# Gates by seven block products in a two-layer graph network kernel, with block sums on GpSimd

## Chip, cores, metric

The kernel runs on one core of a Trainium2 chip. The metric is device time in microseconds, from the core's first to its last instruction; most executions agree within 0.3%. SBUF is the on-chip memory that holds the tiles; PSUM is the one into which TensorE's results go (tiles named ps_). A change of over 2% counts as faster or slower.

## The reference

There are 64 graphs of 256 nodes with 256 features, in fp32. Layer 0, cut to what matters, is a gated update of x. Its inputs are a convolution along the nodes and a message sum:

```python
x_conv = relu(h + xc)                       # two convolutions, the second with 17 taps
x_nmp  = A @ relu(x @ w_msg.T + b_msg)      # A = exp(-dist) * mask
x_in = concatenate([x_conv, x_nmp])         # (256, 512)
gi = x_in @ w_ih.T + b_ih                   # (256, 768), parts r, z, n
gh = x @ w_hh.T + b_hh
r = sigmoid(gi_r + gh_r); z = sigmoid(gi_z + gh_z)
nn_ = tanh(gi_n + r * gh_n)
out = (1 - z) * nn_ + z * x                 # then x = layernorm(x + out)
```

Layer 1 normalizes (the kernel calls that result h), projects, sums over neighbours and normalizes again.

## The kernel before

Graphs are handled in turns, one graph k a turn, in batches of eight. A turn also holds pieces of its neighbours: message sums of k+1, distances of k+2, messages of k+3, projection and aggregation of k-1. `pump()` inserts pieces of the next batch's convolution at ten places of a turn. In these traces each engine runs its instructions in the order of the program. The gates, which the change rewrites:

```python
def gates_rz(k, n):                          # n: half of the nodes
    prz = bank("ps_rz")                      # 512 columns: r and z
    for c in range(C):
        nc.tensor.matmul(prz, XT[k][:, c, q], whh[:, c, 0:2 * D], start=(c == 0), stop=False)
    for i, t in enumerate(ins):              # xc (2 chunks), nmp (2 chunks)
        nc.tensor.matmul(prz, t, wih[:, i, 0:2 * D], start=False, stop=(i == 3))
    nc.vector.tensor_add(rz[:, n, :], prz, brzn[:, :2 * D])
    nc.scalar.activation(rz[:, n, :], rz[:, n, :], AF.Tanh, scale=0.5)
# gates_n(k, n): the same with 256 columns for each of the two n parts, and one addition

def update(k):                               # ... statistics of w on VectorE, small powers on GpSimd
    for n in range(C):
        nc.vector.tensor_scalar(H[k][:, n, :], w[:, n, :], mv[:, n, 0:1], q[:, 1, n:n + 1],
                                ALU.subtract, ALU.mult)
    # ... X1 by two ScalarE activations

for k in range(b * BG, (b + 1) * BG):        # a turn, cut
    load(k + 3); load_x(k + 1)               # the transfers, at its start
    gates_rz(k, 0); pump(); gates_n(k, 0); pump()
    transposes_h(k - 1); pump(); gates_rz(k, 1); pump(); passing(k + 1); pump()
    factors(k + 2); gates_n(k, 1); pump(); project(k - 1)
    # ... update(k), distances(k + 2), messages(k + 3), mask(k + 2), aggregate(k - 1)
```

## Time and profile before

| | before |
|---|---|
| time, median of 4 runs | 2313.66 us |
| TensorE busy | 2225 us, 96% |
| VectorE busy | 1685 us, 73% |
| GpSimd busy | 469 us, 20% |
| a turn without convolution work for TensorE | 25.6 us |
| a batch of eight turns | 272 us |

The lines themselves stand in the prediction. "Busy" is time in which an engine runs instructions. Idle time matters only on the engine that bounds a stage, so shares are read by stage, here by turn. A group's line gives its instructions' total busy time, their mean in ns, and the idle time before them with what ended it.

I measure turns from one start of the transposes of h on TensorE to the next. The heavy stage is the first six of the eight intervals so cut in a batch, where VectorE carries most of the next convolution; the light stage is the other two.

### The profile page before, as it was taken

Reading aid. Unit: us, or ns where it says so; the run is one execution under the profiler, and the core shown is the slowest. Engines: PE = TensorE matmul, PEld = TensorE weight load, DVE = VectorE, ACT = ScalarE, POOL = GpSimd, SP = SyncE. Lnnn points to the kernel's source line nnn. Section 1 sums busy time; section 2 is a strip of 40 time slices with the busy share of each in tenths; the row PEclk is TensorE's granted clock in tenths of the full one; section 3 lists DMA queues with packets and bytes.
Section 4 is the critical chain, followed back from the end, with each engine's and each line's share of the span. In section 5 each row is a group of like instructions: output and inputs, shape, how many; then the busy total and the mean of one; then the engine's idle time right before and its main releaser. Section 6 shows DMA issues by size and latency. Waiting matters only on the chain.

```text
span 2314.6 us, 24215 instructions
## 1 busy us (share of the span) xinstructions
PE 2225.2 (96%) x8262; PEld 1456.2 (63%) x8262; DVE 1685.2 (73%) x3212; ACT 766.0 (33%) x1577; POOL 468.7 (20%) x925
## 2 busy tenths in 40 slices
PE   7879999999999999999999999999999999999996
PEld 4565566666666666666666566665666656666663
DVE  2893998759794788829887498956889398874543
ACT  4514222442224321353224332253223532243332
POOL 1000221312122222202212131221222122121211
PEclk8998999999999999999999999999999999999998
DMA  5543152224323144221532234222433214321100
GB/s 176 156 161 114 59 170 67 85 94 130 118 73 109 50 137 132 74 100 37 169 99 73 101 106 143 75 96 69 136 105 101 94 43 151 113 78 37 46 23 14
DMA packets 211128, 226.66 MB, mean 98 GB/s; under 512 B 22087, under 2 KB 201790, under 8 KB 211006
## 3 DMA queue, kind: packets, MB, share of 16 engines
q1 hardware_dynamic: 188448, 191.14, 26.2%
q10 hardware_dynamic: 22558, 33.99, 4.2%
q8 instruction: 66, 1.08, 0.2%
q14 instruction: 56, 0.46, 0.1%
HBM read 179.22 MB, written 45.88 MB: 97 GB/s over the span
## 4 chain that ended last, share of the span: by engine, by line
PE 69%; DVE 21%; DMA 4%; issue 3%; POOL 2%; ACT 1%; ACTq 0%; SPq 0%; DVEq 0%; POOLq 0%
PE ps_rz L637 14%; PE ps_k L383 12%; DVE XF L103 8%; PE ps_n L649 7%; PE ps_rz L635 7%; PE ps_out L712 6%; PE ps_c L454 5%; PE ps_nmp L619 4%; PE ps_n L647 4%; PE ps_out L724 3%; PE ps_msg L575 3%; DVE w L103 2%; DVE XF L464 2%; DVE bst L654 2%; DMA w<-w2m 2%
## 5 line engine op out<-in xcount | busy, mean ns | idle before, releaser
L103 DVE SCALAR_TENSOR_TENSOR XF<-XF 128x512 f32<-128x512 f32 (+2 forms) x800 | 506.7, 664 | 7.0
L676 POOL TENSOR_SCALAR q<-mv 128x2 f32<-128x2 f32 x64 | 32.1, 502 | 1459.1 <-DVE mv L655 1459.1
L383 PE MATMUL ps_k<-w,XF 128*128 128x256 f32 x1316 | 302.1, 385 | 15.2 <-ACT AT L609 11.6
L383 PEld LDWEIGHTS ps_k<-w,XF 128*128 128x128 f32 x1316 | 248.5, 192 | 64.1 <-ACT AT L609 17.3
L650 DVE TENSOR_TENSOR gn<-ps_n,brzn 128x512 f32<-128x512 f32 x128 | 88.1, 688 | 239.4 <-PE ps_n L649 239.4
L641 ACT ACTIVATE rz<-rz 128x512 f32<-128x512 f32 x128 | 80.7, 631 | 509.9 <-DVE rz L640 509.9
L635 PE MATMUL ps_rz<-whh,xT 128*128 128x512 f32 x512 | 240.8, 592 | 0.0
L637 PE MATMUL ps_rz<-wih,xc 128*128 128x512 f32 x512 | 240.6, 592 | 0.0
L637 PE MATMUL ps_rz<-wih,nmp 128*128 128x512 f32 x512 | 240.6, 592 | 0.0
L712 PE MATMUL ps_out<-wrr,hT 128*128 128x512 f32 x512 | 232.8, 598 | 5.5 <-ACT hT L701 5.5
L640 DVE TENSOR_TENSOR rz<-ps_rz,brzn 128x512 f32<-128x512 f32 x128 | 87.2, 681 | 192.2 <-PE ps_rz L637 192.2
L637 PEld LDWEIGHTS ps_rz<-wih,nmp 128*128 128x128 f32 x512 | 97.3, 190 | 122.5 <-issue 122.5
L637 PEld LDWEIGHTS ps_rz<-wih,xc 128*128 128x128 f32 x512 | 97.2, 190 | 122.5 <-issue 121.5
L712 PEld LDWEIGHTS ps_out<-wrr,hT 128*128 128x128 f32 x512 | 98.1, 192 | 105.2 <-issue 89.6
L580 ACT ACTIVATE msg<-msg 128x512 f32<-128x512 f32 x64 | 40.4, 631 | 353.1 <-DVE msg L579 353.1
L575 PE MATMUL ps_msg<-wms,xT 128*128 128x260 f32 x512 | 134.1, 402 | 12.5 <-DMA adj<-in_adjT_dram 8.1
L635 PEld LDWEIGHTS ps_rz<-whh,xT 128*128 128x128 f32 x512 | 92.2, 190 | 64.5 <-issue 61.2
L647 PE MATMUL ps_n<-whh,xT 128*128 128x256 f32 x512 | 131.6, 379 | 0.0
L649 PE MATMUL ps_n<-wih,xc 128*128 128x256 f32 x512 | 131.4, 379 | 0.0
L649 PE MATMUL ps_n<-wih,nmp 128*128 128x256 f32 x512 | 131.4, 379 | 0.0
L360 DVE TENSOR_TENSOR XF<-XF 128x512 f32<-128x512 f32 (+3 forms) x128 | 125.2, 1004 | 1.8
L454 PE MATMUL ps_c<-xTc,w 128*128 128x512 f32 x256 | 118.1, 604 | 7.6 <-ACT xTc L446 7.6
(105 smaller groups left out, 3486.6 us busy)
## 6 DMA issues: line engine op xcount, KB each, us to landing
w<-w2m SPq DMA_DIRECT2D x105, 768.0 KB, 5.9
xn<-in_x_dram SPq DMA_DIRECT2D x32, 512.0 KB, 4.3
xt<-xTc ACTq DMA_DIRECT2D x32, 512.0 KB, 3.3
xT<-xt SPq DMA_DIRECT2D x64, 256.0 KB, 3.0
adj<-in_adjT_dram SPq DMA_DIRECT2D x64, 256.0 KB, 2.8
x<-in_x_dram SPq DMA_DIRECT2D x64, 256.0 KB, 3.1
xb<-in_x_dram SPq DMA_DIRECT2D x32, 512.0 KB, 4.9
out_dram<-y ACTq DMA_DIRECT2D x64, 256.0 KB, 2.2
```

The costliest lines, as they stand in the source:

```text
L103: nc.vector.scalar_tensor_tensor(o, in0, s, in1, op0=op0, op1=op1)
L360: (nc.vector.tensor_add if add else nc.vector.tensor_sub)(sl(o, n), sl(a, n), sl(b, n))
L383: nc.tensor.matmul(ps, X[:, slot, c * P:(c + 1) * P], w(m, c), start=(c == 0), stop=(c == C - 1))
L454: nc.tensor.matmul(ps, w1[:, c, o * P:(o + 1) * P], xTc[:, c, :], start=(c == 0), stop=(c == C - 1))
L575: nc.tensor.matmul(ps[:, :D + 4], XT[k][:, c, m * P:(m + 1) * P], wms[:, c, :], start=(c == 0), stop=(c == C - 1))
L619: nc.tensor.matmul(ps[:, d * N:(d + 1) * N], MSG[k][:, m, d * P:(d + 1) * P], AT[k][:, m, :], start=(m == 0), stop=(m == C - 1))
L635: nc.tensor.matmul(prz, XT[k][:, c, q], whh[:, c, 0:2 * D], start=(c == 0), stop=False)
L637: nc.tensor.matmul(prz, t, wih[:, i, 0:2 * D], start=False, stop=(i == 3))
L647: nc.tensor.matmul(pn[:, D:], XT[k][:, c, q], whh[:, c, 2 * D:], start=(c == 0), stop=(c == C - 1))
L649: nc.tensor.matmul(pn[:, :D], t, wih[:, i, 2 * D:], start=(i == 0), stop=(i == 3))
L650: nc.vector.tensor_add(RZ[k][1][:, n, :], pn, brzn[:, 2 * D:])
L712: nc.tensor.matmul(ps, hT[:, c, n * P:(n + 1) * P], wrr[:, c, :], start=(c == 0), stop=(c == C - 1))
```

## The change

The gates become a 2 x 2 block product over node halves and feature chunks, done with seven products in place of eight (a Strassen-type scheme: four sums of blocks on each side come first, and save one product). The weights' sums are made once. The left sums are made per graph on GpSimd, for x, xc and nmp. A product has 384 columns (a third each of r, z and n) for nmp and xc, and 256 for x. Bank sums replace some additions. h moves from VectorE to ScalarE. To make room, x is updated in place and the ring of xc is shorter; the loads move from the start of a turn to its middle.

```diff
+    def blocks(src, s1, s2, s3, s4):
+        a11, a12, a21, a22 = (src[:, c, n * P:(n + 1) * P] for n in range(C) for c in range(C))
+        nc.gpsimd.tensor_add(s1, a21, a22)
+        nc.gpsimd.tensor_sub(s2, s1, a11)
+        nc.gpsimd.tensor_sub(s3, a11, a21)
+        nc.gpsimd.tensor_sub(s4, a12, s2)
+        return a11, a12, s4, a22, s1, s2, s3
 ...
+        a = bank("ps_a")
+        block_product(k, 0, a, True)
+        nc.scalar.copy(g00, a[:, :HG])
+        d = bank("ps_d")
+        block_product(k, 1, d, True)
+        nc.vector.tensor_add(g00, g00, d[:, :HG])
+        nc.gpsimd.tensor_add(g00, g00, bg[:, 1, :])
 ...  (products 4 and 6 into banks b_ and c_)
+        block_product(k, 5, a, False)
+        nc.vector.tensor_add(g.rearrange("p n h e -> p (n h) e")[:, 1:3, :],
+                             a[:, :HG].unsqueeze(1).to_broadcast([P, 2, HG]), bg)
+        nc.gpsimd.tensor_add(g11, g11, g01)
 ...  (product 2 onto b_, added into g01; product 3 onto c_, added into g10; tanh after each)
-        for n in range(C):
-            nc.vector.tensor_scalar(H[k][:, n, :], w[:, n, :], mv[:, n, 0:1], q[:, 1, n:n + 1],
-                                    ALU.subtract, ALU.mult)
+        for i, dst in ((1, H[k]), (0, w)):
+            for n in range(C):
+                nc.scalar.activation(dst[:, n, :], w[:, n, :], AF.Identity, ...)
 ...
+            load(k + 3); load_adj(k + 2); load_x(k + 1)      # after the third gate step
```

More of the change, by code (lines that the diff above doesn't have):

```diff
@@ L31 @@
 NB = B // BG
+RING = 10
+HG = 3 * P
 PI = math.pi
@@ L128, in gnn_two_layers @@
     tb_dram = nc.inline_tensor(np.ascontiguousarray(tb), name="tap_matrix")
-    tap_sb = const.tile([TAPS * OB, NM * OB], F32)
-    nc.scalar.dma_start(out=tap_sb, in_=tb_dram.ap())
     mhalf = const.tile([P, 8], F32)
@@ L169, in filters @@
     def filters(pool):
+        tap_sb = pool.tile([TAPS * OB, NM * OB], F32, name="tap_sb")
+        nc.scalar.dma_start(out=tap_sb, in_=tb_dram.ap())
         W2[0] = pool.tile([P, C, NM, D], F32, name="w2all")
@@ L520, in conv @@
             yield cost(2)
-        xcs = [work.tile([P, C, 4, N], F32, tag="xc", name="xc", bufs=3) for _ in range(2)]
+        if "xc" not in XC:
+            XC["xc"] = work.tile([P, RING, C, N], F32, name="xc", bufs=1)
+        ring, at = XC["xc"], b * BG % RING
+        spans = [(0, min(BG, RING - at), at)]
+        if spans[0][1] < BG:
+            spans.append((spans[0][1], BG, 0))
         def channels(q):
@@ L529, in channels @@
                 pv = ps.rearrange("p (j g t) -> p j g t", j=4, g=BG)
-                for h in range(2):
+                for g0, g1, r in spans:
                     nc.scalar.activation(
-                        xcs[h][:, o].rearrange("p g (t j) -> p j g t", j=M)[:, 4 * q:4 * q + 4],
-                        pv[:, :, 4 * h:4 * h + 4, :], AF.Relu)
+                        ring[:, r:r + g1 - g0, o].rearrange("p g (t j) -> p j g t", j=M)[:, 4 * q:4 * q + 4],
+                        pv[:, :, g0:g1, :], AF.Relu)
                 yield 1.0
@@ L548, in conv, with load_adj @@
         for g in range(BG):
-            XC[b * BG + g] = (xcs[g // 4], g % 4)
-    XG, ADJ, XT, NMP, AT, MSG, X1, H, ST, RZ, OUTS = ({} for _ in range(11))
+            XC[b * BG + g] = ring[:, (b * BG + g) % RING]
+    XG, ADJ, XT, NMP, AT, MSG, X1, H, ST, G, GN, LEFT, OUTS = ({} for _ in range(13))
     def load(k):
-        if k >= B:
-            return
-        XT[k] = work.tile([P, C, N], F32, tag="xT", name="xT", bufs=4)
-        nc.sync.dma_start(out=XT[k], in_=xt_dram[k // 2][:, :, (k % 2) * N:(k % 2 + 1) * N])
-        ADJ[k] = work.tile([P, C, N], F32, tag="adj", name="adj", bufs=5)
-        nc.sync.dma_start(out=ADJ[k], in_=adjT[k].rearrange("(c p) n -> p c n", p=P))
+        if k < B:
+            XT[k] = work.tile([P, C, N], F32, tag="xT", name="xT", bufs=4)
+            nc.sync.dma_start(out=XT[k], in_=xt_dram[k // 2][:, :, (k % 2) * N:(k % 2 + 1) * N])
+    def load_adj(k):
+        if k < B:
+            ADJ[k] = work.tile([P, C, N], F32, tag="adj", name="adj", bufs=4)
+            nc.sync.dma_start(out=ADJ[k], in_=adjT[k].rearrange("(c p) n -> p c n", p=P))
     def load_x(k):
         if k < B:
-            XG[k] = work.tile([P, C, D], F32, tag="x", name="x")
+            XG[k] = work.tile([P, C, D], F32, tag="x", name="x", bufs=3)
             nc.sync.dma_start(out=XG[k], in_=x[k].rearrange("(c p) d -> p c d", p=P))
     def messages(k):
-        MSG[k] = work.tile([P, C, D], F32, tag="msg", name="msg", bufs=3)
+        MSG[k] = work.tile([P, C, D], F32, tag="msg", name="msg")
         st = sts[k % len(sts)]
@@ L621, in passing @@
         nc.scalar.copy(NMP[k].rearrange("p c n -> p (c n)"), ps)
-    def inputs(k, n):
-        xc, g = XC[k]
-        q = slice(n * P, (n + 1) * P)
-        return q, (xc[:, 0, g, q], xc[:, 1, g, q], NMP[k][:, 0, q], NMP[k][:, 1, q])
-    def gates_rz(k, n):
-        if n == 0:
-            RZ[k] = (work.tile([P, C, 2 * D], F32, tag="rz", name="rz", bufs=1),
-                     work.tile([P, C, 2 * D], F32, tag="gn", name="gn", bufs=1))
-        q, ins = inputs(k, n)
-        prz = bank("ps_rz")
-        for c in range(C):
-            nc.tensor.matmul(prz, XT[k][:, c, q], whh[:, c, 0:2 * D], start=(c == 0), stop=False)
-        for i, t in enumerate(ins):
-            nc.tensor.matmul(prz, t, wih[:, i, 0:2 * D], start=False, stop=(i == 3))
-        rz = RZ[k][0]
-        nc.vector.tensor_add(rz[:, n, :], prz, brzn[:, :2 * D])
-        nc.scalar.activation(rz[:, n, :], rz[:, n, :], AF.Tanh, scale=0.5)
@@ L643, in gates_n @@
-    def gates_n(k, n):
-        q, ins = inputs(k, n)
-        pn = bank("ps_n")
-        for c in range(C):
-            nc.tensor.matmul(pn[:, D:], XT[k][:, c, q], whh[:, c, 2 * D:], start=(c == 0), stop=(c == C - 1))
-        for i, t in enumerate(ins):
-            nc.tensor.matmul(pn[:, :D], t, wih[:, i, 2 * D:], start=(i == 0), stop=(i == 3))
-        nc.vector.tensor_add(RZ[k][1][:, n, :], pn, brzn[:, 2 * D:])
+    def blocks(src, s1, s2, s3, s4):
[5 more added lines that the diff above has]
+        return a11, a12, s4, a22, s1, s2, s3
@@ new lines, in sums, with block_product @@
+    def sums(k, name):
+        if name == "x":
+            src = XT[k]
+            t = work.tile([P, 4, P], F32, name="xsum", bufs=1)
+            s3 = t[:, 3, :]
+        else:
+            src = {"nmp": NMP, "xc": XC}[name][k]
+            t = work.tile([P, 3, P], F32, name=name + "sum", bufs=1)
+            s3 = src[:, 0, P:]
+        LEFT[k, name] = blocks(src, t[:, 0, :], t[:, 1, :], s3, t[:, 2, :])
+    def block_product(k, i, ps, start):
+        for j, (name, w) in enumerate((("nmp", wg[:, i, 1, :]), ("x", wx[:, i, :]), ("xc", wg[:, i, 0, :]))):
+            nc.tensor.matmul(ps[:, :w.shape[-1]], LEFT[k, name][i], w, start=start and j == 0, stop=j == 2,
+                             skip_group_check=not start)
@@ new lines, in gates @@
+    def gates(k):
+        g = work.tile([P, C, 2, HG], F32, name="g", bufs=1)
+        G[k] = g
+        g00, g01, g10, g11 = (g[:, n, h, :] for n in range(C) for h in range(2))
+        a = bank("ps_a")
[5 more added lines that the diff above has]
+        nc.gpsimd.tensor_add(g00, g00, bg[:, 1, :])
+        yield
+        b_ = bank("ps_b")
+        block_product(k, 4, b_, True)
+        nc.scalar.copy(g11, b_[:, :HG])
+        c_ = bank("ps_c")
+        block_product(k, 6, c_, True)
+        nc.vector.tensor_add(g11, g11, c_[:, :HG])
+        yield
+        block_product(k, 5, a, False)
+        nc.vector.tensor_add(g.rearrange("p n h e -> p (n h) e")[:, 1:3, :],
+                             a[:, :HG].unsqueeze(1).to_broadcast([P, 2, HG]), bg)
+        nc.gpsimd.tensor_add(g11, g11, g01)
+        yield
+        block_product(k, 2, b_, False)
+        nc.vector.tensor_add(g01, g01, b_[:, :HG])
+        nc.scalar.activation(g[:, 0, :, :2 * P], g[:, 0, :, :2 * P], AF.Tanh, scale=0.5)
+        yield
+        block_product(k, 3, c_, False)
+        nc.vector.tensor_add(g10, g10, c_[:, :HG])
+        nc.scalar.activation(g[:, 1, :, :2 * P], g[:, 1, :, :2 * P], AF.Tanh, scale=0.5)
+        yield
@@ L652, in stats, with gates_n @@
+    def gates_n(k):
+        ps = bank("ps_n")
+        for n in range(C):
+            for c in range(C):
+                nc.tensor.matmul(ps[:, n * D:(n + 1) * D], XT[k][:, c, n * P:(n + 1) * P], wn[:, c, :],
+                                 start=(c == 0), stop=(c == C - 1))
+        GN[k] = work.tile([P, C, D], F32, name="gn", bufs=1)
+        nc.vector.tensor_add(GN[k], ps.rearrange("p (n d) -> p n d", n=C), bn_.unsqueeze(1).to_broadcast([P, C, D]))
     def stats(mv, k, src):
@@ L657, in update @@
     def update(k):
-        rz, gn = RZ[k]
-        nn = work.tile([P, C, D], F32, tag="nn", name="nn", bufs=1)
-        stt(nn, rz[:, :, :D], 1.0, gn[:, :, D:], op0=ALU.add, op1=ALU.mult)
-        stt(nn, nn, 0.5, gn[:, :, :D])
+        g, w, nn = G[k], XG[k], GN[k]
+        parts = nn.rearrange("p n (h e) -> p n h e", h=2)
+        stt(nn, g[:, :, 0, :2 * P], 1.0, nn, op0=ALU.add, op1=ALU.mult)
+        stt(parts, parts, 0.5, g[:, :, :, 2 * P:])
         nc.scalar.activation(nn, nn, AF.Tanh)
         yield
-        w = work.tile([P, C, D], F32, tag="w", name="w", bufs=1)
-        nc.vector.tensor_sub(w, XG[k], nn)
-        stt(w, rz[:, :, D:], 3.0, w, op0=ALU.add, op1=ALU.mult)
+        nc.vector.tensor_sub(w, w, nn)
+        stt(w, g[:, :, 1, :2 * P], 3.0, w, op0=ALU.add, op1=ALU.mult)
         stt(w, nn, 4.0, w)
@@ L678, in update @@
         nc.gpsimd.tensor_tensor(q, q, mhalf[:, :2 * C].rearrange("p (a c) -> p a c", a=2), ALU.pow)
-        sh = work.tile([P, C], F32, tag="sh", name="sh", bufs=4)
-        nc.gpsimd.tensor_mul(sh, mv[:, :, 0], q[:, 0, :])
+        sh = work.tile([P, 2, C], F32, tag="sh", name="sh", bufs=4)
+        nc.gpsimd.tensor_mul(sh, mv[:, :, 0].unsqueeze(1).to_broadcast([P, 2, C]), q)
         nc.gpsimd.tensor_scalar(sh, sh, -1.0, None, ALU.mult)
@@ L683, in update @@
         H[k] = work.tile([P, C, D], F32, tag="h", name="h", bufs=1)
-        X1[k] = work.tile([P, C, D], F32, tag="x1", name="x1", bufs=2)
-        for n in range(C):
-            nc.vector.tensor_scalar(H[k][:, n, :], w[:, n, :], mv[:, n, 0:1], q[:, 1, n:n + 1],
-                                    ALU.subtract, ALU.mult)
-        for n in range(C):
-            nc.scalar.activation(X1[k][:, n, :], w[:, n, :], AF.Identity, bias=sh[:, n:n + 1], scale=q[:, 0, n:n + 1])
+        for i, dst in ((1, H[k]), (0, w)):
+            for n in range(C):
+                nc.scalar.activation(dst[:, n, :], w[:, n, :], AF.Identity,
+                                     bias=sh[:, i, n:n + 1], scale=q[:, i, n:n + 1])
+        X1[k] = w
         yield
@@ L778, in gnn_two_layers @@
         nc.sync.dma_start(out=brel, in_=rows[:, R_REL:R_REL + D].to_broadcast([P, D]))
-        brzn = const.tile([P, 4 * D], F32)
-        nc.sync.dma_start(out=brzn[:, :3 * D], in_=rows[:, R_IH:R_IH + 3 * D].to_broadcast([P, 3 * D]))
-        nc.sync.dma_start(out=brzn[:, 3 * D:], in_=rows[:, R_HH + 2 * D:R_HH + 3 * D].to_broadcast([P, D]))
-        bhh = first_pool.tile([P, 2 * D], F32, name="bhh")
-        nc.sync.dma_start(out=bhh, in_=rows[:, R_HH:R_HH + 2 * D].to_broadcast([P, 2 * D]))
+        bg = const.tile([P, 2, HG], F32)
+        bhh = first_pool.tile([P, 2, 2 * P], F32, name="bhh")
+        for i, h in ((0, 1), (1, 0)):
+            for t, at, src in ((bg[:, i, :2 * P], h * D, R_IH), (bg[:, i, 2 * P:], 2 * D + h * P, R_IH),
+                               (bhh[:, i, :], h * D, R_HH)):
+                n = t.shape[-1]
+                nc.sync.dma_start(out=t, in_=rows[:, src + at:src + at + n].to_broadcast([P, n]))
+        bn_ = const.tile([P, D], F32)
+        nc.sync.dma_start(out=bn_, in_=rows[:, R_HH + 2 * D:R_HH + 3 * D].to_broadcast([P, D]))
         gb = const.tile([P, 2, C], F32)
         nc.sync.dma_start(out=gb, in_=rows[:, R_GAMMA:R_GAMMA + 2 * D].rearrange("o (v c p) -> p (o v) c", p=P, c=C))
-        whh = weight(whhT, D, 3 * D, "whh", nc.sync)
         wrr = const.tile([P, C, 2 * D], F32)
@@ L800, in gnn_two_layers @@
             pass
-        nc.vector.tensor_add(brzn[:, :2 * D], brzn[:, :2 * D], bhh)
+        nc.vector.tensor_add(bg[:, :, :2 * P], bg[:, :, :2 * P], bhh)
         nc.gpsimd.tensor_scalar(wrr, wrr, 0.5, None, ALU.mult)
@@ L807, in gnn_two_layers, with weight_sums @@
     work = ctx.enter_context(tc.tile_pool(name="work", bufs=2))
-    wih = weight(wihT, 2 * D, 3 * D, "wih", nc.sync, work)
     for k in range(3):
         load(k)
+        if k < 2:
+            load_adj(k)
     load_x(0)
+    wg = work.tile([P, 7, 2, HG], F32, name="wg", bufs=1)
+    wx = work.tile([P, 7, 2 * P], F32, name="wx", bufs=1)
+    wn = work.tile([P, C, D], F32, name="wn", bufs=1)
+    ih, hh = wihT.rearrange("(s c p) n -> c p s n", c=C, p=P), whhT.rearrange("(c p) n -> c p n", p=P)
+    for i, c, h in ((0, 0, 0), (1, 1, 0), (2, 1, 1), (4, 0, 1)):
+        nc.sync.dma_start(out=wg[:, i, :, :2 * P], in_=ih[c, :, :, h * D:(h + 1) * D])
+        nc.sync.dma_start(out=wg[:, i, :, 2 * P:], in_=ih[c, :, :, 2 * D + h * P:2 * D + (h + 1) * P])
+        nc.sync.dma_start(out=wx[:, i, :], in_=hh[c, :, h * D:(h + 1) * D])
+    nc.sync.dma_start(out=wn, in_=hh[:, :, 2 * D:].rearrange("c p n -> p c n"))
+    def weight_sums(*which):
+        for i, j, l in which:
+            for w in (wg, wx):
+                nc.gpsimd.tensor_sub(w[:, i], w[:, j], w[:, l])
     early = [lambda: messages(0), lambda: messages(1), lambda: factors(0), lambda: distances(0), lambda: mask(0),
-             lambda: factors(1), lambda: distances(1), lambda: mask(1), lambda: passing(0), lambda: messages(2)]
+             lambda: factors(1), lambda: distances(1), lambda: mask(1), lambda: passing(0), lambda: messages(2),
+             lambda: sums(0, "x"), lambda: weight_sums((6, 2, 4), (4, 4, 0)), lambda: sums(0, "nmp"),
+             lambda: weight_sums((5, 2, 4), (3, 1, 5))]
     mark = total
@@ L821, in gnn_two_layers @@
         f()
+    sums(0, "xc")
     POINTS = 10
@@ L838, in gnn_two_layers @@
         for k in range(b * BG, (b + 1) * BG):
-            load(k + 3)
-            load_x(k + 1)
-            up = update(k)
+            ga, up = gates(k), update(k)
             agg = None
-            gates_rz(k, 0)
+            step(ga)
             pump()
-            gates_n(k, 0)
+            step(ga)
             step(y_left)
@@ L850, in gnn_two_layers @@
             pump()
-            gates_rz(k, 1)
+            step(ga)
+            load(k + 3)
+            load_adj(k + 2)
+            load_x(k + 1)
             pump()
+            step(ga)
             if k + 1 < B:
@@ L855, in gnn_two_layers @@
             pump()
+            step(ga)
+            if k + 1 < B:
+                sums(k + 1, "x")
+                if (k + 1) % BG:
+                    sums(k + 1, "xc")
+                sums(k + 1, "nmp")
             if k + 2 < B:
                 factors(k + 2)
-            gates_n(k, 1)
+            gates_n(k)
             pump()
@@ L881, in gnn_two_layers @@
             pass
+        if b + 1 < NB:
+            sums((b + 1) * BG, "xc")
     step(y_left)
```

## The prediction

> **What bounds the kernel now.** I read the page's busy table and slices first, then the chain, then the groups by line and shape, then busy times in fixed stretches, then single instructions in order of time.
>
> ```profile
> PE 2225.2 (96%) x8262; PEld 1456.2 (63%) x8262; DVE 1685.2 (73%) x3212; ACT 766.0 (33%) x1577; POOL 468.7 (20%) x925
> PE   7879999999999999999999999999999999999996
> DVE  2893998759794788829887498956889398874543
> PE 69%; DVE 21%; DMA 4%; issue 3%; POOL 2%; ACT 1%; ACTq 0%; SPq 0%; DVEq 0%; POOLq 0%
> ```
>
> TensorE is the bound: after the prologue (three slices) its row is nines to the end. Busy time can flatter it, since matmuls overlap, so I looked at the pitch in the chain that ended last, in order of time:
>
> ```profile
> 192.07 3.43 PE ps_rz L637 x8
> 290.10 10.60 PE ps_k L383 x48
> 308.01 5.18 PE ps_k L383 x24
> ```
>
> Eight 512-column fp32 instructions take 3.43 us, so 428.5 ns each; 24 of 256 columns take 5.18 us, 215.8 ns each. That is 0.83 ns a column plus some 3 ns: the stream runs without holes, and its price is columns, not instructions. Every fp32 matmul is two such instructions (512 in a group for 4 per graph by 64 graphs).
>
> VectorE must be read by stage. The kernel handles 64 graphs in batches of 8; during a batch the next batch's convolution is spread through the turns. Busy times in 17 us stretches of one batch (about 272 us long), columns the stretch, its length, PE, PEld, DVE, ACT, POOL (busy us and instructions), clock, DMA share, GB/s:
>
> ```profile
> 787.00:804.00 17.00, 17.00 (x62) 10.79 (x61) 16.66 (x23) 6.67 (x14) 2.16 (x4) 1.00 0.19 62
> 838.00:855.00 17.00, 17.00 (x71) 12.53 (x70) 16.62 (x28) 4.29 (x8) 2.36 (x2) 1.00 0.60 198
> 889.00:906.00 17.00, 17.00 (x64) 11.71 (x63) 10.29 (x21) 3.65 (x8) 0.00 (x0) 1.00 0.47 157
> 1008.00:1025.00 17.00, 16.41 (x60) 9.46 (x59) 2.92 (x7) 7.97 (x16) 1.86 (x6) 1.00 0.49 172
> ```
>
> From 770 to 974 us (six of the eight turns) VectorE sums to 183 us of 204, in several stretches 97 or 98%, while TensorE sums to 201.5. From 974 to 1042 (two turns) VectorE is busy only 25 us of 68. So TensorE is the bound everywhere, but in the heavy stage VectorE is right behind it. After the last convolution, the last eight graphs run with VectorE about half busy and TensorE full.
>
> **What the skill says, against this trace.** (1) The Trainium skill, "SBUF — State Buffer", section "Who interferes with whom": VectorE's second port pair is shared with GpSimd; a VectorE instruction with two SBUF inputs contends with a GpSimd instruction that reads SBUF, and the later one blocks until the first is done. The trace agrees on one side:
>
> ```profile
> 564.11 2.23 POOL L736 TENSOR_TENSOR sh<-mv,q 128x2 f32<-128x2 f32 x1
> 566.43 2.27 POOL L737 TENSOR_SCALAR sh<-sh 128x2 f32<-128x2 f32 x1
> 564.01 7.00 DVE L360 TENSOR_TENSOR XF<-XF 128x2048 f32<-128x2048 f32 x4
> ```
>
> A two-column GpSimd operation, 0.20 us when undisturbed (its minimum is 196 ns), lasts 2.23 us beside a 2.29 us VectorE addition, and the next again: GpSimd waits out one VectorE instruction, then gets a turn. The other side, VectorE held up, is not visible, for GpSimd's operations here are 2 to 6 columns wide. (2) "GPSIMD Engine Reference", section "Performance versus the Vector engine": a two-input fp32 addition over 2048 columns takes 4497 ns on GpSimd, 2.2 ns a column. This trace's only wide GpSimd operations, one-input, took 2793 ns (1024 columns) and 862 ns (256): 2.5 ns a column plus 0.22 us; I use these. (3) "TensorE: Matmul & The Clock Gate", section "Wait — 56ns, not 53.3ns?": start to start is N over 2.4 GHz plus some 2.5 ns when warm. The 428.5 ns above are 2 x 512 / 2.4 plus 1.8 ns, so the form agrees, with two passes per fp32 instruction.
>
> **The change, part by part.**
>
> TensorE. The groups:
>
> ```profile
> L635 PE MATMUL ps_rz<-whh,xT 128*128 128x512 f32 x512 | 240.8, 592 | 0.0
> L637 PE MATMUL ps_rz<-wih,xc 128*128 128x512 f32 x512 | 240.6, 592 | 0.0
> L637 PE MATMUL ps_rz<-wih,nmp 128*128 128x512 f32 x512 | 240.6, 592 | 0.0
> L649 PE MATMUL ps_n<-wih,xc 128*128 128x256 f32 x512 | 131.4, 379 | 0.0
> ```
>
> Before, a graph needs 12 matmuls of 512 columns and 12 of 256 for its gates: 9216 columns. After: seven block products of 384 + 256 + 384 columns, and 4 matmuls of 256 for the hidden n part: 7168 + 1024 = 8192. Saved: 1024 columns in two instructions each, 2 x 1024 x 0.83 = 1.71 us a graph, 109 us in 64. Matmuls go from 24 to 25, which costs nothing. Weight loads (190 ns) stay below the 384-column stream (some 322 ns). Ceiling: 4.7%.
>
> VectorE. Groups of 256 and 512 columns take 415 and 685 ns, so 0.146 us plus 1.05 ns a column. Before: four gate additions of 512 (2.74 us) and two h instructions (0.82): 3.56 us. After: four of 384 (0.55 each), one of 768 (0.95), one of 512 (0.69): 3.84 us. Net +0.28 us a graph, +18 us in all. It also stops waiting for GpSimd before h (41.4 us in the waits), but gains a wait: its addition into g01 must follow GpSimd's reading of g01.
>
> GpSimd. Twelve block sums of 128 columns (0.54 us each) and two additions of 384 (1.18): 8.8 us a graph, 565 us in all, from 20% to about 46% before waits. Of this 2304 columns x 2.5 ns = 5.8 us a graph is streaming, in which it may hold the shared port.
>
> ScalarE. Two PSUM copies of 384 (0.48 us, between the 373 ns for 256 and 586 for 512) and h (2 x 0.59): +2.1 us a graph, from 33% to about 40%. Harmless as a load, but h now follows GpSimd's last small operation, two ScalarE instructions later than the chain did.
>
> Loads mid-turn: they land in about 3 us with half a turn left. Hidden before, hidden after. Prologue: the weight pieces, their sums on GpSimd and more transfers ahead of the convolution's last inputs add perhaps 5 us.
>
> **Sum and rivals.**
>
> A, TensorE stays the bound and all 109 us arrive, less the 5: about 2210. For: TensorE is 96% busy. Against: in the heavy stage VectorE needs 183 + 2 of what would be 194 us, with stretches at 98% where a faster TensorE can gain only half a microsecond a turn. I take off 15 to 20 us even without contention: 2225.
>
> B, VectorE becomes the bound because GpSimd's sums hold the shared port. About two thirds of VectorE's work has two SBUF inputs, so each turn can lose up to 0.65 x 5.8 = 3.8 us. Then the heavy stage is 185 + 6 x 3.8 = 208 us plus about 8 of VectorE's own waits, 216 against 204 before: 12 lost in each of seven batches, 84 us. Safe gains remain: two light turns in seven batches (7 x 2 x 1.71 = 24 us) and the last eight graphs (14 us). Sum 2314 + 84 - 38 + 5 = 2365. Against: an in-order GpSimd queue often runs beside PSUM-source or one-input VectorE work, and VectorE sheds h.
>
> C, half of that contention, 1.5 us a turn: the heavy stage 185 + 9 + 8 = 202 against 204. The safe 38 us stay, plus 14, less 5: about 2267.
>
> D, a new wait: h arrives late. Between the last gate matmul and the transposes of h lie on TensorE now about 14.6 us (project 3.4, distances 0.9, messages 1.7, aggregate 1.7, four block products 6.9), before 15.5, and the chain grew by ScalarE's two h instructions and by block sums queued ahead of GpSimd's statistics. TensorE may wait 0 to 2 us a turn, 0 to 80 us. It comes with B, not in addition to it.
>
> **Range and chances.** The mechanism on TensorE is sure, the loss to port contention and late VectorE is not. Between A corrected (2225), C (2267) and B (2365), with the first two much likelier, because the change plainly takes work off VectorE, I put the middle at 2255 us (-2.6%), and 2200 to 2345 as the range. Faster by over 2% means below 2268: 0.53. Within 2%: 0.33. Slower: 0.14.
>
> **What would show it.** TensorE columns: block products of 384 columns in groups at about 322 ns pitch, TensorE busy down by about 105 us (if its share also falls below 94%, the gain turned into waits). GpSimd at about 1000 us busy or more, block sums well above 0.54 us in the heavy stage where they wait for VectorE. VectorE: two-input instructions of 512 columns longer than the present 685 ns mean B; equal means A. The waits: TensorE at the transposes on h (7.2 us now) shows D; VectorE on GpSimd at g01 shows the new order. In the last eight graphs each turn should be 1.7 us shorter whatever else happens. The prediction is wrong if GpSimd's long reads block VectorE fully, or not at all.

## The result

The changed kernel takes 2330.81 us (median of 4 runs) against 2313.66. A ratio here is the mean time of one kernel's runs over that of the other's of the same rounds, so not quite the ratio of the medians quoted. It is 1.0071, with a 95% interval of 1.0048 to 1.0093: slower by 0.7%. The time lies inside the stated range of 2200 to 2345, but the forecast gain (2255, 59 us less) did not come; "within 2%" had been given a chance of 0.33.

The busy table, the rows of TensorE and VectorE by slices, and the shares of the chain that ended last, from the page of the changed kernel:

```profile
PE 2150.1 (92%) x8390; PEld 1485.2 (64%) x8390; DVE 1807.1 (78%) x3212; ACT 872.0 (37%) x1809; POOL 1044.0 (45%) x1829
PE   7877899999999999999999999999899999999997
DVE  3992999849996699948998399975999579994454
PE 42%; DVE 40%; issue 6%; POOL 5%; ACT 3%; DMA 3%; SPq 0%; ACTq 0%; POOLq 0%; DVEq 0%
```

TensorE fell to 92%: its lighter work turned into waiting. The chain, 69% TensorE and 21% VectorE before, is now shared between the two. VectorE's busy time rose by 122 us, where its instructions account for 18. TensorE's mean granted clock was 0.979 against 0.984, but its 256-column instructions take 382 ns in both traces, so the clock is not the cause.

Instructions of the last graphs in order of time (start, us, engine), then VectorE's groups by shape (the first from the kernel before, the others after), and GpSimd's two additions:

```profile
2167.36 0.81 PE L657 MATMUL ps_a<-wg,nmp 128*128 128x384 f32 x2
2168.00 0.59 PE L657 MATMUL ps_a<-wx,xT 128*128 128x256 f32 x2
...
L103 DVE SCALAR_TENSOR_TENSOR XF<-XF 128x512 f32<-128x512 f32 x448 | 294.5, 686 | 5.0
L105 DVE SCALAR_TENSOR_TENSOR XF<-XF 128x512 f32<-128x512 f32 x448 | 334.3, 771 | 5.0
L682 DVE TENSOR_TENSOR g<-ps_a,bg 128x768 f32<-128x768 f32 x64 | 61.0, 952 | 64.8 <-PE ps_a L657 64.8
...
L684 POOL TENSOR_TENSOR g<-g 128x384 f32<-128x384 f32 x64 | 79.6, 1243 | 397.6 <-DVE g L682 397.6
L672 POOL TENSOR_TENSOR g<-g,bg 128x384 f32<-128x384 f32 x64 | 69.2, 1081 | 16.4 <-DVE g L671 16.4
```

Two 384-column instructions take 0.64 us, 0.32 each, as forecast. VectorE's two-input instructions over SBUF (L105) went from 686 to 771 ns for the same shape, while the one with a PSUM source (L682) takes the 0.95 us that the columns say. A place in a heavy turn shows why, again in order of time:

```profile
977.52 0.68 DVE L105 SCALAR_TENSOR_TENSOR XF<-XF 128x512 f32<-128x512 f32 x1
...
978.99 2.08 DVE L105 SCALAR_TENSOR_TENSOR XF<-XF 128x512 f32<-128x512 f32 x2
979.15 1.37 POOL L684 TENSOR_TENSOR g<-g 128x384 f32<-128x384 f32 x1 [3.90 <-DVE g L682]
```

Two VectorE instructions that need 1.4 us take 2.08 beside one GpSimd addition, and the addition itself takes 1.37 instead of 1.00.

Where the time went, by turn (mean of five middle batches, us, worked out from the view in order of time):

| interval in a batch | 1 | 2 | 3 | 4 | 5 | 6 | 7 | 8 | sum |
|---|---|---|---|---|---|---|---|---|---|
| before | 25.6 | 36.6 | 43.7 | 42.0 | 25.6 | 28.2 | 27.4 | 42.8 | 271.9 |
| after | 28.3 | 38.5 | 41.6 | 40.1 | 24.8 | 32.0 | 27.6 | 41.7 | 274.6 |
| before less 1.71 each | 23.9 | 34.9 | 42.0 | 40.3 | 23.9 | 26.5 | 25.7 | 41.1 | 258.2 |

The first transposes of h start at 248.8 us instead of 238.5 (+10.3). The seven batches from there take 1901.5 us instead of 1884.8 (+16.8); the rest, the last graphs, 176.8 instead of 191.3 (-14.5). These add up, before rounding, to the 12.5 us by which the profiled spans differ. The last graphs, without convolution work, run at 23.9 us a turn instead of 25.6, exactly the columns' worth. One batch by stage, before first and after second (the first six intervals; length, then TensorE, its weight loads, VectorE, ScalarE, GpSimd, each busy us and instructions, clock, DMA share, GB/s):

```profile
782.00:984.00 202.00, 199.52 (x750) 134.02 (x749) 180.00 (x350) 57.25 (x119) 50.32 (x92) 0.99 0.32 103
795.00:1001.00 206.00, 194.07 (x767) 137.87 (x767) 194.63 (x347) 69.57 (x148) 111.39 (x178) 0.98 0.33 106
```

VectorE's busy time there is now as long as TensorE's. So the arithmetic works, and something in the batches takes it back.

### The profile page after: what moved, and what is told of

It is laid out like the page before. It is cut to its first block, busy times and chain, and to the rows that moved or that the text cites. A ratio compares the mean times of both kernels' runs of the same rounds, so it can differ in the third digit from the quotient of the medians.

```text
span 2327.1 us, 25882 instructions
## 1 busy us (share of the span) xinstructions
PE 2150.1 (92%) x8390; PEld 1485.2 (64%) x8390; DVE 1807.1 (78%) x3212; ACT 872.0 (37%) x1809; POOL 1044.0 (45%) x1829
## 4 chain that ended last, share of the span: by engine, by line
PE 42%; DVE 40%; issue 6%; POOL 5%; ACT 3%; DMA 3%; SPq 0%; ACTq 0%; POOLq 0%; DVEq 0%
DVE XF L105 12%; PE ps_k L385 7%; PE ps_c L657 5%; PE ps_b L657 5%; PE ps_a L657 4%; DVE XF L362 4%; PE ps_c L456 4%; DVE x L105 3%; PE ps_n L701 3%; PE ps_nmp L628 3%; DVE bst L708 3%; PE ps_out L765 2%; DVE XF L466 2%; PE ps_out L777 2%; DVE gn L105 2%
## 5 line engine op out<-in xcount | busy, mean ns | idle before, releaser
L105 DVE SCALAR_TENSOR_TENSOR XF<-XF 128x512 f32<-128x512 f32 (+2 forms) x800 | 572.4, 743 | 6.8
L684 POOL TENSOR_TENSOR g<-g 128x384 f32<-128x384 f32 x64 | 79.6, 1243 | 397.6 <-DVE g L682 397.6
L628 PE MATMUL ps_nmp<-AT,msg 128*128 128x256 f32 x512 | 122.8, 383 | 1.1 <-DVE AT L621 1.1
L584 PEld LDWEIGHTS ps_msg<-wms,xT 128*128 128x128 f32 x512 | 95.6, 196 | 42.0 <-issue 19.4
L777 PE MATMUL ps_out<-hr,adj 128*128 128x256 f32 x512 | 121.9, 380 | 0.1
L701 PE MATMUL ps_n<-wn,xT 128*128 128x256 f32 x512 | 121.1, 379 | 0.0
L657 PE MATMUL ps_b<-wg,xcsum 128*128 128x384 f32 x256 | 105.1, 492 | 16.9 <-POOL xcsum L638 16.9
L628 PEld LDWEIGHTS ps_nmp<-AT,msg 128*128 128x128 f32 x512 | 98.3, 192 | 28.8 <-issue 1.8
L754 ACT ACTIVATE hT<-ps_hT,gb 128x256 f32<-128x256 f32 x128 | 65.0, 558 | 123.9 <-PE ps_hT L752 110.6
L682 DVE TENSOR_TENSOR g<-ps_a,bg 128x768 f32<-128x768 f32 x64 | 61.0, 952 | 64.8 <-PE ps_a L657 64.8
L657 PE MATMUL ps_b<-wg,nmpsum 128*128 128x384 f32 x256 | 106.1, 497 | 3.6 <-DVE y L779 2.3
```

The costliest lines, as they stand in the source:

```text
L105: nc.vector.scalar_tensor_tensor(o, in0, s, in1, op0=op0, op1=op1)
L584: nc.tensor.matmul(ps[:, :D + 4], XT[k][:, c, m * P:(m + 1) * P], wms[:, c, :], start=(c == 0), stop=(c == C - 1))
L628: nc.tensor.matmul(ps[:, d * N:(d + 1) * N], MSG[k][:, m, d * P:(d + 1) * P], AT[k][:, m, :], start=(m == 0), stop=(m == C - 1))
L657: nc.tensor.matmul(ps[:, :w.shape[-1]], LEFT[k, name][i], w, start=start and j == 0, stop=j == 2, skip_group_check=not start)
L684: nc.gpsimd.tensor_add(g11, g11, g01)
L701: nc.tensor.matmul(ps[:, n * D:(n + 1) * D], XT[k][:, c, n * P:(n + 1) * P], wn[:, c, :], start=(c == 0), stop=(c == C - 1))
```

## The experiments

Theory 1: GpSimd's reads take the port that VectorE needs for a second SBUF input, and VectorE is the bound in the heavy turns, so blocked time becomes kernel time. Theory 2: GpSimd's results come late in its in-order queue, and TensorE waits for them. Theory 3: the order of ScalarE's queue ties TensorE to late VectorE additions. Each run is given as its ratio to the kernel before from the same rounds. Where I speak of us between runs, it is the difference of ratios times 2314.

**Writes in place of the block sums** (wrong result).

```diff
-        nc.gpsimd.tensor_add(s1, a21, a22)
+        nc.gpsimd.memset(s1, 0.0)
+        nc.gpsimd.memset(s1, 0.0)
         # the same for s2, s3, s4
```

> The changed kernel with each of GpSimd's twelve block sums per graph replaced by two memsets of the same block (wrong result on purpose): GpSimd stays occupied about as long (24 x 0.32 = 7.7 us a graph against 8.7 measured) and the block products still wait for GpSimd, but it reads nothing from SBUF there; the two 384-column additions stay. Theory 1 (GpSimd's reads hold the port that VectorE needs for its second SBUF input, and VectorE is the bound in the heavy turns): VectorE's 512-column two-input instructions fall from 771 ns to about 700, VectorE busy from 1807 to about 1725 us, time to about 2250 us. Theory 2 (GpSimd's results come late in its in-order queue, and TensorE waits for them): VectorE may speed up, but the time stays above 2300 us.

2301.93 us, ratio 0.9953: 27 us less than the change. VectorE busy 1758 us (from 1807), its 512-column instructions 739 ns (from 771). Theory 1 missed its size: the reads of the block sums are worth 27 us, not 80. Theory 2's mark of 2300 is met by 2 us, which settles nothing. A memset took 0.205 us, not the 0.32 that I had assumed, so GpSimd was also less occupied (837 us against 1044); but the two places where TensorE meets late sums (next run) did not move, so the 27 us are not lateness there.

**No block sums at all** (wrong): the lines above removed, and the products take a11, a12, a12, a22, a21, a11, a21.

> The changed kernel with the block sums left out, the products taking plain blocks of the same size instead (wrong result on purpose); the two additions of 384 columns stay. Theory 1: within 10 us of the run with memsets, about 2245 us. Theory 2: clearly faster than the run with memsets, by 30 us or more, since the lateness is gone only here.

2276.17 us, ratio 0.9842: another 26 us, with VectorE's durations the same as in the run before, 739 ns. So these 26 us, short of the 30 of theory 2, are lateness, not contention. The turns show where: the first transposes of h start at 239.9 us (248.7 with memsets), and interval 7 takes 25.7 us (27.6); the waits of the changed kernel name the sum:

```profile
PE ps_b L657 <- POOL xcsum L638: 16.9, 8, 5.3
```

That is 9 + 7 x 1.9 = 22 us, at the start and at each batch's first graph, whose sums of convolved channels can be made only when the batch's convolution ends. Theory 2 holds there; the heavy stage has the other 4 us (201.1 to 200.5 a batch). But 739 ns still is not 685: two GpSimd additions were left.

**The disputed cost alone, in the kernel before.** Twelve additions of 128 columns and two of 384 per graph on GpSimd, into a scratch tile that nobody reads; and the same with memsets.

```diff
+    def extra(dst, a, b):
+        nc.gpsimd.tensor_add(dst, a, b)      # second run: nc.gpsimd.memset(dst, 0.0)
```

> The kernel before with the disputed cost alone: twelve 128-column and two 384-column two-input additions per graph on GpSimd, into a scratch tile that nobody reads, in the same places of the program as in the changed kernel. Result stays right. Theory 1: VectorE's 512-column two-input instructions go from 685 to about 770 ns, VectorE busy from 1685 to about 1790 us; TensorE was the bound by a small margin, so the time rises by 15 to 60 us. Theory 2 (nothing waits for these results): time and VectorE's durations unchanged, within 5 us.

> As the run with reads, but the fourteen GpSimd operations are memsets of the same widths: GpSimd's instructions and its queue are loaded, without reads. Theory 1: VectorE's durations and the time as in the kernel before, within 5 us. If GpSimd's mere activity or its writes cost anything, this shows it: time up as in the run with reads.

With reads: 2344.41 us, ratio 1.0136, slower by 31 us, result right. With writes: 2313.25, ratio 1.0003. VectorE's groups by shape, with reads first and with writes second:

```profile
L103 DVE SCALAR_TENSOR_TENSOR XF<-XF 128x512 f32<-128x512 f32 x448 | 334.9, 775 | 5.0
```
```profile
L103 DVE SCALAR_TENSOR_TENSOR XF<-XF 128x512 f32<-128x512 f32 x448 | 294.4, 685 | 5.0
```

Nothing depends on these results, and VectorE's wait for GpSimd's own small results is unchanged (41.3 us with reads, 41.4 with writes, 41.4 before). The writes occupied GpSimd for less time than the reads (166 us more than before, against 607). But if occupation alone did it, they would have cost VectorE some 31 us (an estimate, 166/607 of 115), and they cost none. So the effect is the reads themselves: VectorE busy 1800.6 us against 1684.4. This shows theory 1's mechanism without any of the change around it.

**No added GpSimd work at all** (wrong): the run without block sums, and without the two 384-column additions.

> The run without block sums, and without the two 384-column additions on GpSimd as well (wrong result on purpose): GpSimd does only what it did in the kernel before. Theory 1 (port contention): VectorE's 512-column two-input instructions back at 685 ns (739 with only the two additions left), VectorE busy about 1700 us, the time falls by another 20 to 40 us from 2276 to about 2245. If the contention is the only loss, it falls to about 2215. Theory 3 (what is left is a wait by queue order: the second half's tanh stands in ScalarE's queue ahead of the copies that the distances need): TensorE's wait for lr stays above 15 us, and the time stays above 2235.

2231.13 us, ratio 0.9625. The busy table, and VectorE's group:

```profile
PE 2120.1 (95%) x8390; PEld 1477.7 (66%) x8390; DVE 1703.2 (76%) x3212; ACT 875.2 (39%) x1809; POOL 415.2 (19%) x933
```
```profile
L105 DVE SCALAR_TENSOR_TENSOR XF<-XF 128x512 f32<-128x512 f32 x448 | 295.6, 685 | 5.0
```

VectorE is back at 685 ns and 1703 us, 18 more than before, as the prediction had it. TensorE's busy time is 105 us below the kernel before. The two additions alone were worth 50 us of time (0.9842 to 0.9625) and 55 us of VectorE, more than the twelve block sums' 49 us, with half the columns (768 against 1536). Not all of the 50 us need be the port: VectorE's wait for GpSimd before its addition into g01 (15.1 us) goes too, and no run has memsets in the place of these two. All of GpSimd's added work costs 4.5 points of ratio, 103 us. Theory 3 misses both its marks, the second narrowly: the wait for the distances is 7.7 us, below its 15, and the time below its 2235.

**Theory 3: the distances' copies earlier.**

```diff
             if k > 0:
                 transposes_h(k - 1)
+            if k + 2 < B:
+                factors(k + 2)
             pump()
 ...
-            if k + 2 < B:
-                factors(k + 2)
             gates_n(k)
```

> The changed kernel with the two ScalarE copies for the coming distances (and their transposes) issued right after the transposes of h, ahead of the tanh instructions, not behind them; result stays right. Theory 3 (ScalarE's queue order ties TensorE to late VectorE additions): TensorE's wait at the distances (25.8 us) vanishes and the time falls by 10 to 30 us, to about 2310. Rival (VectorE is the bound in these turns, and that wait is only where TensorE meets it): the wait moves elsewhere, above all to the transposes of h, and the time stays within 5 us of 2331.

2335.93 us, ratio 1.0083: no gain. TensorE's longest waits, in the changed kernel first and in this one second (waiting, what ended it, us in total, times, longest):

```profile
PE ps_hT L752 <- ACT h L740: 28.2, 42, 5.5
PE ps_dist L616 <- ACT lr L607: 25.8, 25, 2.5
```
```profile
PE ps_hT L752 <- ACT h L740: 37.9, 31, 5.5
```

The wait at the distances is gone and the one at the transposes of h has grown: TensorE meets late VectorE in another place. Theory 3 falls, and its rival holds.

**VectorE with more work: h back on it.**

```diff
-                nc.scalar.activation(dst[:, n, :], w[:, n, :], AF.Identity, ...)   # H[k]
+            nc.vector.tensor_scalar(H[k][:, n, :], w[:, n, :], mv[:, n, 0:1], q[:, 1, n:n + 1],
+                                    ALU.subtract, ALU.mult)
```

> The changed kernel with h back on VectorE (two one-input instructions, 0.75 us a graph), the rest as changed; result right. If VectorE's throughput bounds the heavy turns (five of eight): slower by about 0.75 x 35 = 26 us, 2350 to 2360. If the length of the chain from GpSimd's statistics over ScalarE to the transposes of h bounds them (TensorE waits 28 us there): faster by 10 to 25 us.

2409.4 us, ratio 1.0396: 75 us slower than the change, three times what I expected. VectorE's busy time grew by 44 us (1850.8), and in its queue it now waits for GpSimd in front of h:

```profile
DVE h L739 <- POOL q L731: 41.3, 50, 1.7
```

I had counted the instructions and not the waits. But the 75 us are not the sum of 44 and 41, for VectorE's waits for ScalarE fell by as much (from 117 to 76 us). By stage, VectorE's busy time rose by 6.9 us in the heavy intervals of a batch (194.2 to 201.1) and their length by 8.9 (205.3 to 214.2), as if VectorE were the bound; the light stage, where it is not, lost another 2.4 us, of which TensorE's longer wait for the late sums (28.4 us in all, 16.9 in the change) is 1.6. Without the move of h to ScalarE the change would have been 75 us slower.

**The two additions on VectorE.** The bias goes in with the block that ScalarE copied before (PSUM source), and g11 += g01 moves as it is.

> The changed kernel with the two 384-column additions moved from GpSimd to VectorE (the bias goes into the block that ScalarE copied before, so that copy goes too); result right. From the run without GpSimd's additions the contention of these two is worth 45 us of time; the two VectorE instructions cost 2 x 0.55 us a graph, 70 us of VectorE in all, of which the heavy turns feel some 60%, 42 us. So if VectorE's time in the heavy turns is the bound, whether it is used or blocked, this comes out within 10 us of 2331. If the additions hurt in another way (late results on GpSimd), it falls by 30 us or more.

2336.57 us, ratio 1.0083: no better. VectorE busy 1829 us; its 512-column instructions are at 739 ns. In the heavy intervals VectorE is busy for as long as in the change, so blocked or used, the time is VectorE's either way. Put together (mean of five middle batches, us a batch):

| heavy stage | VectorE busy | length |
|---|---|---|
| no added GpSimd work | 179.3 | 194.4 |
| no block sums | 187.3 | 200.5 |
| memsets for block sums | 187.4 | 201.1 |
| the change | 194.2 | 205.3 |
| two additions on VectorE | 194.5 | 207.1 |
| h on VectorE | 201.1 | 214.2 |
| the kernel before | 180.3 | 201.7 |

In the changed kernels the length follows VectorE's busy time and lies 11 to 15 us above it. In the kernel before it lies 21 us above, and 2.8 us above TensorE's (198.9).

**The rest of the change alone.** Eight plain block products, four VectorE additions, no sums; all else as changed.

> The changed kernel with eight plain block products and one VectorE addition for each of the four blocks, without block sums, copies and GpSimd additions; all else of the change stays (h on ScalarE, loads mid-turn, the ring, weights by blocks). Result right. If the rest of the change costs nothing: TensorE's columns are those of the kernel before, so about 2310 to 2318 us, with the first transposes of h some 5 us late at most. If the moved loads or h on ScalarE cost something, it is above 2325.

2333.43 us, ratio 1.0071. So the change without its seven products costs 16 us, above what I expected. Interval 8 is 45.2 us instead of 42.8, which makes most of it; TensorE waits there for the transposed channels 2.1 us instead of 0.6, and for h. In the changed kernel interval 8 is only 0.6 us above the columns' worth, so this is a small part of its loss. In this layout, then, seven products with GpSimd's sums gain nothing over eight plain ones (both 1.0071), while seven without added GpSimd work (0.9625) take 103 us less, near the 109 us of the columns. **The loads at the start of the turn again** was meant to settle it, in three kernels:

```diff
+            load(k + 3)
+            load_adj(k + 2)
+            load_x(k + 1)
             ga, up = gates(k), update(k)
 ...  (removed after the third gate step)
```

> The plain block products in the changed layout, with the loads of coming graphs back at the start of the turn. If the mid-turn loads cause the 2.4 us that the eighth turn of each batch loses: 14 us faster, about 2319. If it is ScalarE's queue (h and x after one another, ahead of the copies of the transposed channels), unchanged at about 2333.

> The changed kernel with the loads back at the start of the turn. The eighth turn there is already at its columns' worth (41.7 against 41.1 us), so the loads should cost nothing: within 5 us of 2331. If loads issued at the start of the turn get in the way of the convolution's weights in the heavy turns, slower by over 5 us, which would be why they were moved.

> The best hybrid with the loads back at the start of the turn: as the changed kernel, within 5 us of the hybrid's 2274; faster only if the plain layout's loss shows in its plain turns too.

2391.96 us (1.0341), 2391.08 (1.0331) and 2342.62 (1.0119): all about 60 to 70 us slower, against every expectation but one side remark. The waits say why; TensorE in the changed kernel with early loads:

```profile
PE ps_k L385 <- DMA w<-w2m: 60.6, 22, 5.6
```

In the changed kernel this wait is 0.4 us. The loads' buffers come free only when VectorE and TensorE finish an earlier graph. At the start of a turn the loads stand waiting in their queue (the one for x 61 times on VectorE's y, 48 times when mid-turn), and the convolution's weights wait behind them. In the kernel before the loads also stood at the start of the turn, but the one for x waited 9 times, 60 us in all (309 us here), and TensorE waited 2.5 us for the weights. So in the changed kernel the loads had to move; that the update of x in place is the reason fits these waits, but no run tests it alone. What costs the plain layout its 2.4 us in interval 8 stays open.

**A hybrid.** Seven products only where VectorE has slack, in graphs 0, 3, 4 and 7 of each eight and in the last eight; plain products elsewhere. Two buffers shrink to make room for a fourth plain weight block.

```diff
+SEVEN = (0, 3, 4, 7)
+    def seven(k):
+        return k >= B - BG or (k > 0 and k % BG in SEVEN)
-            ga, up = gates(k), update(k)
+            ga, up = (gates if seven(k) else gates_plain)(k), update(k)
```

> Seven products only in the turns in which VectorE has slack (graphs 0, 3, 4 and 7 of each eight, and the last eight graphs), plain block products in the others, and the copies for the distances early; result right. If VectorE's shortage and the contention in the heavy turns are what ate the gain: the light turns keep 1.7 to 2.3 us each, 7 x 4 x 1.9 = 53 us and 14 us at the end, so about 2250 to 2265. If not, within 1% of the kernel before.

> The hybrid (seven products in graphs 0, 3, 4, 7 of each eight and in the last eight) with the copies for the distances in the place that the change has: in the changed kernel issuing them early cost 5 us, so here about 2277; if the order matters only where VectorE is late, as in the turns that are plain here, within 3 us of 2281.

> As that, but graph 0 of each eight plain as well: its sums of the convolved channels come at the very end of the batch, and TensorE waited 11.7 us for them in seven turns. It loses 7 x 1.7 = 12 us of columns and saves that wait: within 5 us of the other hybrid. If the late sums also hold up VectorE there, faster by 10 us.

With the distances' copies early: 2281.43 us, ratio 0.9845. With them where the change has them: 2273.9, ratio 0.9814 (0.9799 to 0.9829). With graph 0 plain too: 2289.34, ratio 0.988; its interval 8 is 45.2 us again, the plain layout's. The first two came out above my 2250 to 2265, and dropping graph 0 was 15 us slower where I expected no loss. The middle one beats both kernels, by 1.9% ("unclear" at the 2% mark) and 2.5%. Its intervals are 26.1, 36.2, 41.3, 40.1, 25.6, 28.6, 27.6 and 41.4 us. In intervals 1, 2 and 6 it avoids the change's loss, and where it uses seven products it keeps the gain. This supports theory 1's second half: where VectorE has slack, the seven products pay.

## Why the prediction was wrong

Read against its own steps:

- TensorE's columns: right. The last turns are 1.7 us shorter, 384 columns take 0.32 us, and busy time without added GpSimd work falls by 105 us.
- VectorE's own work: right, +18 us. GpSimd: right in the sum (1044 us busy), partly by luck: alone, a block sum takes 0.45 us and not 0.54, a 384-column addition 1.00 and not 1.18, and blocking made up for it.
- The mechanism of rival B, the shared port: right, shown by the runs with reads and with writes. The skill's rule ("SBUF — State Buffer", section "Who interferes with whom") holds on both sides, with its exception for operations that only write: 1684.4 us of VectorE with memsets, 1685.2 before.
- The weight on A and C was wrong, and in C this term of the sum: "half of that contention, 1.5 us a turn: the heavy stage 185 + 9 + 8 = 202 against 204." The average contention was of that size (1807 - 1703 = 104 us, 1.6 a graph), but it does not spread. In the five middle batches, VectorE's busy time in the six heavy intervals is 194.2 us with GpSimd's work and 179.3 without, 15 us or 2.5 a turn, between C's 1.5 and B's 3.8; in the two light ones it is 31.1 us in both. The contention falls where VectorE is busy, which is where it is the bound. VectorE's other time there is 11 us a batch (205.3 less 194.2) where I had put 8. The heavy stage became 205.3 us, not 202. It had been 201.7, not 204: the prediction's stretches of 17 us did not begin and end with the turns.
- The "safe" light turns were not safe: "two light turns in seven batches" should have saved 3.4 us a batch, and in the table above they save 0.9, because the first graph's sums come late (27.6 us in place of 25.7 without sums). The prologue cost 10.3 us, not 5; 9 of them are block sums again.
- Rival D, h late, was a place where TensorE waits (28 us) and not a cause, as far as one run tells: removing another such wait moved it there.

Together: C let the heavy stage gain 2 us a batch, and it lost 3.6 (201.7 to 205.3); it let the light one gain 3.4, and it gained 0.9. That is 5.6 + 2.5 = 8.1 us a batch, 57 in seven; with 5 more for the prologue, C's 2267 becomes 2329, against 2331 measured. What I lacked in the weighing is that the heavy stage had two bounds within 10% of each other. Adding 2.5 us a turn to VectorE, which also waits 11 us a batch, made it the slower of the two, and the 1.7 us a turn taken from TensorE did not come through (the third and fourth intervals kept it; the first, second and sixth lost 1.9 to 3.8 us).

## What to carry to other kernels

Before moving elementwise work to an idle engine, ask what it shares with the busy one: here some 9 us a graph on an engine that was 20% busy cost the kernel 103 us: 22 through lateness at the start and at batch starts, and some 80 where it blocked VectorE through a port (of these, up to 15 may be VectorE's wait for one GpSimd result). Judge contention in the stage where the engine that suffers is the bound; an average over the run understates it. And when two engines are near-equal bounds in some turns and far apart in others, apply the trade only where the paying engine has slack.

## What the Trainium skill lacked or had wrong

- "SBUF — State Buffer", section "Who interferes with whom": its rule held, but it says who blocks whom and not what that costs a kernel. Here one 384-column GpSimd addition (1.00 us alone) stretched two VectorE instructions from 1.4 to 2.08 us; per graph, two such additions cost VectorE 0.86 us (55 us in 64 graphs) and twelve of 128 columns 0.77 us (49 us). Taken off in this order, few wide ones cost more than many narrow ones with twice the columns; they also stand elsewhere in the turn. Why, no run here tells.
- "GPSIMD Engine Reference", section "When to use GPSIMD": it advises against elementwise work there because two-input operations are about twice as slow. That was not the price here, and the shared SBUF interfaces, which the page names elsewhere, are missing from this advice: with writes in place of reads the added work was free (ratio 1.0003), with reads it cost 1.4% though no one waited for it. The page's time for a two-input addition agrees (section "Performance versus the Vector engine", 4497 ns for 2048 columns, 2.2 ns a column): 0.45 us for 128 columns and 1.00 for 384 is 2.1 ns a column.
- "DMA: Bandwidth & Descriptors", section "Rules for kernel authors", says to issue a DMA early to overlap it. It lacks the case of a load whose buffer is not yet free: issued half a turn earlier, these loads held up others in their queue, and the kernel took 60 us more.
